# Cross-attention with layer norm on one core: one score visit for two row tiles, a cast moved to GpSimd, and a new order of the steady pairs

## The chip, the cores and the metric

The kernel runs on one core of a Trainium2 chip. Its engines work side by side, each through its own list of instructions in order: TensorE (PE in the profile) multiplies matrices and writes into the accumulation memory PSUM, of which a core has 8 banks; VectorE (DVE), ScalarE (ACT) and GpSimd (POOL) do elementwise work; SyncE (SP) issues most of the DMA transfers. Engines wait for each other through semaphores. The metric is the device time of one execution in microseconds.

## The reference

`x` holds 4 batches of 2048 rows of 512 numbers, `ctx_1024` 4 batches of 77 keys of 512 numbers. There are 16 heads of 32 columns.

```
q = x @ wq;  k = ctx @ wk;  v = ctx @ wv                  # split into 16 heads of 32
scores = q k^T / sqrt(32);  scores = where(mask, -inf, scores)
out = softmax(scores) v @ wo + x
result = (out - mean) / sqrt(var + 1e-5) * gamma + beta
```

Everything is float32. Products with the weight matrices are made from three products of split operands (a rounded high part and the rest, the low part): high by high, high by low, low by high.

## The kernel before

**Tiling.** The 8192 rows are 64 tiles `t` of 128 rows. Two tiles form a pair `n` (tiles 2n and 2n+1), four tiles form a group `g` of 512 rows, for which the transposed input is loaded (`load_xT`), cast to its high part (`cast_xT`, L166, on ScalarE, two casts of 128x1024 a group), and split into its low part (`split_xT`, L170, on GpSimd). `q_visit` (L180) makes a quarter of a group's queries: 12 matmuls of 512 columns into one PSUM bank, which `q_evac` (L194, VectorE) copies out.

**One tile's way.** `scores(t)` (L299) takes four banks and forms 16 heads x 128 rows x 77 keys by 32 small float32 matmuls (32 query columns deep, 64 rows wide; each shows as two instructions). `maxima` (L317) takes, on VectorE, one instruction per head that adds the mask, negates, takes the minimum and copies the scores from PSUM to `pbuf`. `exps` (L335, ScalarE) follows with one exponential per head, which also sums it. `recip` (L345, VectorE) and `normalise` (L350, GpSimd) divide. `transp` (L365, VectorE) turns 32x32 blocks into the buffer `B`, `regroup` (L387, SyncE) moves them by 12 transfers a pair into `PT`, `av` (L412, TensorE) multiplies by the values for a whole pair into two banks, `av_hi` (ScalarE) and `av_lo` (VectorE) split that product, `o_proj` (L502, TensorE, 12 matmuls of 512 columns) applies `wo` into one bank, `residual` (L520) and `moments` (L522, VectorE, then four small GpSimd operations L534 to L537) follow, then `scale` (L543, ScalarE), `affine` (L545, two GpSimd operations) and `store`.

**Order.** The order of all instructions on every engine is the order in which the program text issues them. Tiles 0 to 53 come from a loop (L714) whose turn makes one pair, `u` being its even tile. On TensorE a steady turn is: scores of tile u, `o_proj(u-6)`, a query visit, `av(n-2)`, scores of tile u+1, `o_proj(u-5)`, a query visit. Tiles 54 to 63 and everything left over come from the string `ORDER` (L46), a list of words that `do` (L844) executes one by one: a letter for the operation, a tile number, a part.

**PSUM.** `bank` (L98) hands out the 8 banks in a ring. A pair takes 14: four for each tile's scores, two for query visits, two for `av`, two for `o_proj`.

**The mask.** For each batch (8 pairs) `load_mask` and `mask_bias` make an additive mask in 96 columns from 77 by two VectorE operations, and `mask_min` and `mask_nan` (L289, L293) make a per-row epsilon `nz`, which is 1e-5 or, for a row whose keys are all masked, NaN. `moments` adds `nz` to the variance on GpSimd.

Of the kernel before, what the change touches and what calls it, by code (L numbers as in the profile page):

```python
# [31 lines left out]
GRP = 2 * BLK  # L32
MASKED = -3.0e38
EPS = 1.0e-5
WARM = 8
NPB = 3
KSCALE = 1.0 / HD**0.5
LATE = 48
CUT = 27
HALVES = [slice(0, D // 2), slice(D // 2, D)]  # L40

ORDER = """  # L46
# [22 lines left out]
def xattn_layernorm(  # L69
# [25 lines left out]

    ring, kept, rows, summed = [], set(), {}, set()

    def bank(name):  # L98
# [25 lines left out]
    unit = ident.bitcast(F32R)  # L124
    mhalf, mneg, gates = small[:, 0:2], small[:, 2:4], small[:, 4:5]
    last_st = small[:, 8:20].rearrange("p (n s) -> p n s", n=2)
# [24 lines left out]
    def keys_of(h):  # L151
        return slice(TAIL_K, NK2) if h % 2 == 0 else slice(0, NK)
# [10 lines left out]
    def cast_xT(g, c):  # L163
        if g not in gx:
            gx[g] = [sb.tile([P, NC_D, GRP], F32R, tag=t, name=f"{t}_{g}") for t in ("xth", "xtl")]
        nc.scalar.copy(gx[g][0][:, c : c + 2], fx[g, c])  # L166

# [109 lines left out]
    def load_mask(b):  # L277
        m8 = sb.tile([P, TPB, NK], U8, tag="m8", bufs=1, name=f"m8_{b}")
        nc.sync.dma_start(m8, mask[b])
        mb = sb.tile([P, TPB, NK2], BF16, tag="mb", name=f"mb_{b}")  # L280
        nz = sb.tile([P, TPB], F32, tag="nz", name=f"nz_{b}")
        bat[b] = (mb, nz, m8)

    def mask_bias(b, ts=slice(0, TPB)):
        mb, nz, m8 = bat[b]
        nc.vector.tensor_scalar(mb[:, ts, TAIL_K:], m8[:, ts], MASKED, None, ALU.mult)
        nc.vector.tensor_scalar(mb[:, ts, :TAIL_K], m8[:, ts, NK - TAIL_K :], MASKED, None, ALU.mult)

    def mask_min(b):  # L289
        mb, nz, m8 = bat[b]  # L290
        nc.vector.tensor_reduce(nz, m8, AX.X, ALU.min)

    def mask_nan(b):  # L293
        nz = bat[b][1]
        nc.vector.tensor_scalar(nz, nz, 3.0e38, 10.0, ALU.mult, ALU.mult)
        nc.vector.tensor_scalar(nz, nz, 0.0, EPS, ALU.mult, ALU.add)


    def scores(t):  # L299
        qs = qd[t // 4]  # L300
        nmax[t] = sb.tile([P, H], F32, tag="nm", bufs=3, name=f"nm_{t}")
        sums[t] = sb.tile([P, H], F32, tag="sum", bufs=3, name=f"sum_{t}")
        sc = scs[t] = [bank(f"sc_{t}_{j}") for j in range(GH)]
        for g in range(NG):
            for half in range(0, P, P // 2):
                for j in range(GH):
                    q = slice(HD * j, HD * (j + 1))
                    r0 = (t % 4) * P + half
                    nc.tensor.matmul(  # L309
                        sc[j][half : half + P // 2, g * NK : (g + 1) * NK],  # L310
                        qs[q, g, r0 : r0 + P // 2],
                        kct[q, g, t // TPB, keys_of(j)],
                        start=True,
                        stop=True,
                    )

    def maxima(t, lo, hi):  # L317
        pb = pbuf[t % NPB]
        mb = bat[t // TPB][0]
        nm = nmax[t]  # L320
        for h in HEADS[lo:hi]:
            g, j = divmod(h, GH)
            i = slot(h)
            nc.vector.tensor_tensor_reduce(  # L324
                pb[:, i // 2, (i % 2) * NK : (i % 2 + 1) * NK],
                scs[t][j][:, g * NK : (g + 1) * NK],
                mb[:, t % TPB, keys_of(h)],
                -1.0,
                3.0e38,
                ALU.add,  # L330
                ALU.min,
                accum_out=nm[:, i : i + 1],
            )
# [53 lines left out]
    def regroup(b):  # L387
        for n in range(12):
            regroup_part(b, n, nc.sync)
# [132 lines left out]
    def moments(t):  # L522
        b, tt = divmod(t, 2)
        st = sb.tile([P, 6], F32, tag="st", bufs=3, name=f"st_{t}")
        nc.vector.bn_stats(st, od[t])
# [4 lines left out]
        nc.vector.bn_aggr(mv[:, tt, :], st)  # L530
        nz = bat[t // TPB][1]
        if tt == 1:
            k = (t - 1) % TPB
            nc.gpsimd.tensor_tensor(rn[:, 0, :], mv[:, :, 1], nz[:, k : k + 2], ALU.add)  # L534
            nc.gpsimd.tensor_tensor(rn[:, 0, :], rn[:, 0, :], mhalf, ALU.pow)
            nc.gpsimd.tensor_tensor(rn[:, 1, :], mv[:, :, 0], rn[:, 0, :], ALU.mult)
            nc.gpsimd.tensor_tensor(rn[:, 1, :], rn[:, 1, :], mneg, ALU.mult)  # L537
# [50 lines left out]
    def rsqrt_one(t):  # L588
        mv = mvs[t, 1]
        k = t % TPB  # L590
        eps = bat[t // TPB][1][:, k : k + 1]
        if t in summed:
            nc.gpsimd.tensor_scalar(mv[:, 2:3], mv[:, 1:2], 1.0 / D, eps, ALU.mult, ALU.add)
        else:
            nc.gpsimd.tensor_tensor(mv[:, 2:3], mv[:, 1:2], eps, ALU.add)
        nc.gpsimd.tensor_tensor(mv[:, 2:3], mv[:, 2:3], mhalf[:, :1], ALU.pow)
# [35 lines left out]
    nc.gpsimd.memset(mhalf, -0.5)  # L632
    nc.gpsimd.memset(mneg, -1.0)
    for pb in pbuf:
        nc.gpsimd.memset(pb[:, :, 2 * NK :], 0.0)
# [57 lines left out]
    for m in range(0, NG, 2):  # L693
        keys_evac(pks, m)
    mask_min(0)
    for c in range(0, NC_D, 2):
# [16 lines left out]
    evac = [(0, 0)]  # L713
    for u in range(0, 2 * CUT, 2):  # L714
        n = u // 2
# [59 lines left out]
        if k == TPB - 4 and m + 1 < NB:  # L775
            mask_bias(m + 1)
        if k == TPB - 2 and m + 1 < NB:
            mask_min(m + 1)
            mask_nan(m + 1)

# [14 lines left out]
        if u == 0:  # L795
            mask_nan(0)
            split_wv()
            recip(0)
# [37 lines left out]
        "+": residual, "u": rsqrt_one, "y": centre, "z": finish, "k": scale, "f": affine, "w": store,  # L836
        "v": bias_one, "K": stretch, "G": shift, "p": pool_scale, "I": act_mean, "J": act_squares, "M": keep,
    }
# [5 lines left out]
    def do(op, k, part=0, queue="s"):  # L844
# [34 lines left out]

    for word in ORDER.split():  # L880
        op, (k, part) = word[0], (word[1:] + ".").split(".")[:2]
        queue = part[-1:] if part[-1:].isalpha() else ""
        do(op, int(k), int(part[: len(part) - len(queue)] or 0), queue or "s")

# [47 lines left out]
```

## Time and profile before

| | |
|---|---|
| Time, median of 3 runs (lowest, highest) | 514.41 us (514.13, 518.13) |
| Span of the profiled execution, first to last instruction | 510.7 us, 3.7 us less than the median of the runs |
| TensorE matmuls busy | 502.1 us |
| VectorE busy | 472.1 us |
| ScalarE busy | 471.2 us |
| GpSimd busy | 424.3 us |
| Mean granted TensorE clock | 0.996 |

The runs include what lies before the first and after the last instruction, the span does not; the 3.7 us are taken as fixed. Busy shares are means over the whole span; the stage that matters here is the loop over pairs.

### The profile page before, as it was taken

Reading aid. Unit: us, or ns where it says so; the run is one execution under the profiler, and the core shown is the slowest. Engines: PE = TensorE matmul, PEld = TensorE weight load, DVE = VectorE, ACT = ScalarE, POOL = GpSimd, SP = SyncE. Lnnn points to the kernel's source line nnn. Section 1 sums busy time; section 2 is a strip of 40 time slices with the busy share of each in tenths; the row PEclk is TensorE's granted clock in tenths of the full one; section 3 lists DMA queues with packets and bytes.
Section 4 is the critical chain, followed back from the end, with each engine's and each line's share of the span. In section 5 each row is a group of like instructions: output and inputs, shape, how many; then the busy total and the mean of one; then the engine's idle time right before and its main releaser. Section 6 shows DMA issues by size and latency. Waiting matters only on the chain.

```text
span 510.7 us, 20467 instructions
## 1 busy us (share of the span) xinstructions
PE 502.1 (98%) x6864; PEld 387.3 (76%) x6864; DVE 472.1 (92%) x2574; ACT 471.2 (92%) x2239; POOL 424.3 (83%) x382
## 2 busy tenths in 40 slices
PE   8999999999999999999999999999999999999994
PEld 6987777777777777777777777777777777777784
DVE  6798999899999888989999898889999989999997
ACT  6798999999899999999899999999899999999861
POOL 0659359988799988888989998898889989999894
PEclk9999999999999999999999999999999999999998
DMA  8946867888777888789777897788887778767665
GB/s 304 400 155 150 224 177 197 217 237 221 189 207 201 233 215 224 193 222 246 185 202 218 228 230 192 181 235 230 223 217 192 211 198 234 192 185 216 166 207 207
DMA packets 58280, 109.34 MB, mean 214 GB/s; under 512 B 9203, under 2 KB 10739, under 8 KB 58176
## 3 DMA queue, kind: packets, MB, share of 16 engines
q1 hardware_dynamic: 55776, 103.19, 73.1%
q0 software_dynamic: 1872, 4.20, 2.9%
q8 instruction: 55, 0.90, 0.8%
q10 hardware_dynamic: 528, 0.66, 0.4%
q14 instruction: 49, 0.40, 0.3%
HBM read 41.53 MB, written 16.78 MB: 114 GB/s over the span
## 4 chain that ended last, share of the span: by engine, by line
PE 87%; DVE 5%; DMA 4%; SPq 2%; POOL 1%; issue 1%; ACT 1%; DVEq 0%; POOLq 0%
PE pq L177 30%; PE po L517 29%; PE pa L419 10%; PE sc L309 10%; PE sc L517 3%; DMA PT<-B 2%; DVE B L373 2%; PE pv L243 2%; PE pk L203 1%; SPq L385 1%; DVE pbuf L324 1%; DMA stage_a<-wq 1%; PE pq L669 1%; POOL pbuf L350 0%; DVE q L194 0%
## 5 line engine op out<-in xcount | busy, mean ns | idle before, releaser
L339 ACT ACTIVATE pbuf<-pbuf,nm 128x77 f32<-128x77 f32 x1024 | 352.5, 350 | 15.0 <-DVE nm L324 13.6
L339 ACT ACTIVATION_READ_ACCUMULATOR pbuf<-pbuf,nm 128x1 f32 x1024 | 195.3, 191 | 0.0
L324 DVE CUSTOM_DVE_ANT_0 pbuf<-sc,mb 128x77 f32<-128x77 f32 x1020 | 169.9, 230 | 21.8 <-PE sc L309 21.5
L350 POOL TENSOR_TENSOR pbuf<-pbuf,ri 128x1232 f32<-128x1232 f32 x63 | 142.2, 2258 | 17.8 <-DVE ri L345 11.0
L177 PE MATMUL pq<-xth,wqh 128*128 128x512 f32 (+1 forms) x256 | 98.8, 386 | 0.0
L177 PE MATMUL pq<-xtl,wqh 128*128 128x512 f32 (+1 forms) x256 | 98.0, 383 | 0.0
L177 PE MATMUL pq<-xth,wql 128*128 128x512 f32 (+1 forms) x256 | 97.9, 383 | 0.0
L373 DVE STREAM_TRANSPOSE B<-pbuf 128x1280 f32<-128x1280 f32 x63 | 93.9, 1491 | 0.3
L517 PE MATMUL po<-woh,AH 128*128 128x512 f32 x224 | 93.3, 416 | 0.0
L517 PE MATMUL po<-wol,AH 128*128 128x512 f32 x224 | 87.7, 391 | 0.0
L517 PE MATMUL po<-woh,AL 128*128 128x512 f32 x224 | 86.7, 391 | 0.0
L324 DVE DVE_READ_ACCUMULATOR2_ANT nm<- 128x1 f32 x1024 | 83.2, 81 | 0.0
L547 POOL TENSOR_TENSOR o<-o,gam 128x512 f32<-128x512 f32 x53 | 69.9, 1319 | 14.4 <-ACT o L543 14.4
L548 POOL TENSOR_TENSOR o<-o,bet 128x512 f32<-128x512 f32 x53 | 68.4, 1290 | 4.2
L309 PEld LDWEIGHTS sc<-kct,q 32*64 32x64 f32 x4080 | 51.2, 130 | 23.7 <-issue 21.3
L170 POOL TENSOR_TENSOR xtl<-xtf,xth 128x1024 fp32r<-128x1024 f32 x28 | 67.1, 2398 | 0.0
L309 PE MATMUL sc<-kct,q 32*64 32x77 f32 x4080 | 61.2, 238 | 0.0
L419 PE MATMUL pa<-PT,vsb 96*32 96x256 f32 x960 | 58.2, 382 | 0.7 <-DMA PT<-B 0.3
L177 PEld LDWEIGHTS pq<-xth,wqh 128*128 128x128 f32 x256 | 48.1, 188 | 9.8
L177 PEld LDWEIGHTS pq<-xth,wql 128*128 128x128 f32 x256 | 48.1, 188 | 9.4
L177 PEld LDWEIGHTS pq<-xtl,wqh 128*128 128x128 f32 x256 | 48.1, 188 | 9.1
L517 PEld LDWEIGHTS po<-woh,AH 128*128 128x128 f32 x224 | 42.0, 188 | 12.0 <-DVE nm L324 0.4
(167 smaller groups left out, 707.5 us busy)
## 6 DMA issues: line engine op xcount, KB each, us to landing
PT<-B SPq DMA_DIRECT2D x355, 128.0 KB
xtf<-xT SPq DMA_DIRECT2D x28, 512.0 KB
o<-x SPq DMA_DIRECT2D x56, 256.0 KB
out<-o SPq DMA_DIRECT2D x56, 256.0 KB
PT<-B POOLq DMA_DIRECT2D x16, 128.0 KB, 5.2
o_end<-x SPq DMA_DIRECT2D x7, 256.0 KB
out<-o_end SPq DMA_DIRECT2D x7, 256.0 KB
xtf<-xT SPq DMA_DIRECT2D x4, 256.0 KB
```

The lines of the kernel that those rows point to most:

```text
L170: nc.gpsimd.tensor_tensor(l, fx.pop((g, c)), h.bitcast(F32), ALU.subtract)
L177: nc.tensor.matmul(pq, w[:, c, m * P : (m + 1) * P], r[:, c, rs], start=(n == 0), stop=(n == 11))
L243: nc.tensor.matmul(pv, ctx_s[c][i][:, r, :], v[c], start=(n == 0), stop=(n == 11))
L309: nc.tensor.matmul(sc[j][half : half + P // 2, g * NK : (g + 1) * NK], qs[q, g, r0 : r0 + P // 2], kct[q, g, t // TPB, keys_of(j)], start= ...
L324: nc.vector.tensor_tensor_reduce(pb[:, i // 2, (i % 2) * NK : (i % 2 + 1) * NK], scs[t][j][:, g * NK : (g + 1) * NK], mb[:, t % TPB, keys_ ...
L339: nc.scalar.activation(p, p, AF.Exp, bias=nmax[t][:, i : i + 1], scale=-1.0, accum_out=sums[t][:, i : i + 1])
L350: nc.gpsimd.tensor_tensor(pv, pv, rv.to_broadcast((P, NP, 2, NK)), ALU.mult)
L373: nc.vector.transpose(bt.rearrange("p c q r -> p q c r"), pbuf[t % NPB].rearrange("p q (c r) -> p q c r", c=5),)
L419: nc.tensor.matmul(pas[b, g // 2][HD * j : HD * (j + 1), (g % 2) * BLK : (g % 2 + 1) * BLK], vsb[:, 2 * b // TPB, HD * h : HD * (h + 1)], ...
L517: nc.tensor.matmul(pos[t][:, cols], a[:, c, rs], w[:, c, cols], start=go, stop=done)
L547: nc.gpsimd.tensor_tensor(o, o, gam, ALU.mult)
L548: nc.gpsimd.tensor_tensor(o, o, bet, ALU.add)
```

## The change

1. From pair 3 on (`JOIN` = 6 tiles, `CUT` = 27 pairs), 24 pairs no longer come from the loop but from a second string, `PAIR`, executed once a pair with tile and pair numbers relative to the pair. Pairs 0 to 2 keep the loop, tiles 54 to 63 keep `ORDER`, ahead of which stand three words, `JOINT`.
2. In these pairs the scores of both tiles are formed by `scores_pair` (word `S`) and `scores_rest` (word `D`), which follow one another on TensorE. They take six banks instead of eight: four banks `own` hold six 77-column blocks each, two banks `both` hold four each. `S` issues 48 of the 64 small matmuls, `D` the last 16. A pair takes 12 banks instead of 14.
3. On TensorE a pair is: S, D, `o_proj(2n-6)`, `o_proj(2n-5)`, two query visits, `av(n-2)`. The `av` product's second half and both low parts are taken at the start of the next pair.
4. For groups 4 and up the cast to the high part runs on GpSimd (`tensor_copy`), not on ScalarE.
5. The mask is brought to 96 columns on the host, `mask_bias` is one operation, `mask_min` and `mask_nan` are gone, and epsilon is a constant: `moments` adds it on VectorE with a `tensor_scalar` on 128x2 numbers instead of on GpSimd. A row whose keys are all masked now becomes NaN in another way: the cap on the minimum is 2.9e38 (`CEIL`) instead of 3.0e38, so that all its exponentials are zero and it is divided by a zero sum.

```diff
+PAIR = """
+q4 S L b-3.0 i4 a-3.1 T1.30 b-3.1 T0.1 D k-8 T0.2 T0.0 e0.1 e0.0 T1.31 f-8 O-6 x-3 w-8 T0.3 e0.3 B T1.10 e0.2 j4 O-5
++-6 T1.11 s-6 x-4 Q5 T1.1 r0 +-5 k-7 n0 T1.14 e1.11 s-5 e1.14 T1.3 Q6 f-7 q5 e1.1 g5 V-2 e1.15 t-1 t0 e1.10 e1.3 r1
+a-2.0 P-1 n1 w-7
+"""
+JOINT = """ a24.1 b24.0 b24.1 """
...
-        nc.scalar.copy(gx[g][0][:, c : c + 2], fx[g, c])
+        eng = nc.scalar.copy if g < 4 else nc.gpsimd.tensor_copy
+        eng(gx[g][0][:, c : c + 2], fx[g, c])
...
+    def score(t, g, j, half):
+        q = slice(HD * j, HD * (j + 1))
+        r0 = (t % 4) * P + half
+        return nc.tensor.matmul(
+            scs[t][g, j][half : half + P // 2],
+            qd[t // 4][q, g, r0 : r0 + P // 2],
+            kct[q, g, t // TPB, keys_of(j)],
+            start=True,
+            stop=True,
+        )
+
+    def scores_pair(b):
...
+        own = [bank(f"sc_{b}_{j}") for j in range(GH)]
+        both = [bank(f"sc_{b}_{j}") for j in ("e", "f")]
+        units = []
+        for j in range(GH):
+            mine = [(2 * b, g) for g in range(NG)] + [(2 * b + 1, g) for g in range(NG)]
+            for i, (t, g) in enumerate(mine):
+                bk, at = (own[j], i) if i < 6 else (both[j // 2], 2 * (j % 2) + i - 6)
+                scs[t][g, j] = bk[:, at * NK : (at + 1) * NK]
+            units.append(mine[6:] + mine[:6] if j % 2 == 0 else mine)
+        for i in range(6):
+            for half in range(0, P, P // 2):
+                for j in range(GH):
+                    score(*units[j][i], j, half)
+        held[b] = units
+
+    def scores_rest(b):
+        units = held.pop(b)
+        for i in (6, 7):
+            for js in ((0, 2), (3, 1)):
+                for half in range(0, P, P // 2):
+                    for j in js:
+                        score(*units[j][i], j, half)
...
-            nc.gpsimd.tensor_tensor(rn[:, 0, :], mv[:, :, 1], nz[:, k : k + 2], ALU.add)
+            nc.vector.tensor_scalar(rn[:, 0, :], mv[:, :, 1], EPS, None, ALU.add)
...
-    for u in range(0, 2 * CUT, 2):
+    for u in range(0, JOIN, 2):
...
-            tile_parts[op](k, q4 * part, q4 * part + q4)
+            lo, size = (q4 * part, q4) if part < 10 else (2 * part - 20, 2) if part < 20 else (part - 20, 1)
+            tile_parts[op](k, lo, lo + size)
...
+    for n in range(JOIN // 2, CUT):
+        pair(n)
+    for word in (JOINT + ORDER).split():
+        do(*read(word))
```

The words that the prediction uses: `T` maxima, `e` exponentials, `a` and `b` high and low part of the `av` product, `i` cast, `j` split, `r` reciprocal, `n` normalise, `t` transpose, `+` residual, `s` moments, `k` scale, `f` affine, `Q` and `q` query visit and its copy out, `V` the `av` product, `P` regroup, `w` store. A number after the letter is the tile's or pair's distance from the current one; a part of 0 to 3 means four heads, 10 to 17 two heads, 30 and up one head. `S`, `D`, `O`, `Q` and `V` run on TensorE; `T`, `b`, `+`, `s`, `r`, `t`, `q` on VectorE; `e`, `a`, `k` on ScalarE; `i`, `j`, `f`, `n` on GpSimd; `P`, `w`, `x`, `g` and `L` on SyncE's queue.

More of the change, by code (lines that the diff above doesn't have):

```diff
@@ L96, in xattn_layernorm @@
     ring, kept, rows, summed = [], set(), {}, set()
+    held = {}
     def bank(name):
@@ L306, in scores @@
                 for j in range(GH):
[L307 to L315, printed above, removed]
+                    score(t, g, j, half)
+    def score(t, g, j, half):
[9 more added lines that the diff above has]
+    def scores_pair(b):
+        for t in (2 * b, 2 * b + 1):
+            nmax[t] = sb.tile([P, H], F32, tag="nm", bufs=3, name=f"nm_{t}")
+            sums[t] = sb.tile([P, H], F32, tag="sum", bufs=3, name=f"sum_{t}")
+            scs[t] = {}
+        own = [bank(f"sc_{b}_{j}") for j in range(GH)]
[19 more added lines that the diff above has]
+                        score(*units[j][i], j, half)
     def maxima(t, lo, hi):
@@ L633, in xattn_layernorm @@
     nc.gpsimd.memset(mneg, -1.0)
+    nc.gpsimd.memset(meps, EPS)
     for pb in pbuf:
```

77 lines of the change are left out of this document (43 added, 34 removed).

## The prediction

> **What bounds the kernel now.** I read the page first: the busy shares, then the chain that ended last.
>
> ```profile
> span 510.7 us, 20467 instructions
> PE 502.1 (98%) x6864; PEld 387.3 (76%) x6864; DVE 472.1 (92%) x2574; ACT 471.2 (92%) x2239; POOL 424.3 (83%) x382
> PE 87%; DVE 5%; DMA 4%; SPq 2%; POOL 1%; issue 1%; ACT 1%; DVEq 0%; POOLq 0%
> ```
>
> TensorE holds 87% of the chain. The three others are 83% to 92% busy, so whoever takes work from TensorE soon meets another. The chain in order of time shows the loop from its first to its last score visit, with one query visit between:
>
> ```profile
> 59.80 0.88 PE sc L309 x54
> ...
> 206.84 2.72 PE pq L177 x12
> ...
> 404.21 0.88 PE sc L309 x53
> ```
>
> The score visit at 59.80 is that of tile 6, the one at 404.21 of tile 52: 344.41 us for 23 pairs, **14.974 us a pair**. The 24 pairs that the change rewrites are these and one more. Busy times by stretch, for one such pair between the starts of two `av` products (us; PE, PEld, DVE, ACT, POOL):
>
> ```profile
> 201.16:216.09 14.93, 14.93 (x212) 11.38 (x216) 13.42 (x79) 14.51 (x71) 13.18 (x12) 1.00 0.75 199
> ```
>
> TensorE is busy all of the 14.93, at a granted clock of 1.00. VectorE has 1.5 us to spare a pair, ScalarE 0.4, GpSimd 1.75. A shorter TensorE pair shortens the kernel until one of these, or a loop of waits, is met.
>
> **The change part by part.** *The score visit.* TensorE in order of time, around one visit:
>
> ```profile
> 209.17 0.39 PE L177 MATMUL pq<-xth,wql 128*128 128x512 f32 x1
> 209.49 0.95 PE L309 MATMUL sc<-kct,q 32*64 32x77 f32 x64
> 210.37 0.50 PE L517 MATMUL po<-woh,AH 128*128 128x512 f32 x1
> 210.71 0.39 PE L517 MATMUL po<-wol,AH 128*128 128x512 f32 x1
> ```
>
> A stream of 512-column matmuls takes 2.72 / 12 = 0.227 each. Without the visit the next would have started at 209.17 + 0.227 = 209.40; the stream is back in step at 210.71 - 0.227 = 210.48. The visit costs 1.08 us. Its 64 instructions start within 0.95 - 0.23 = 0.72 (0.23 being one of them), 11.4 ns each; the other **0.36 us** is entry and exit. Two visits a pair pay it twice, S and D together once: 128 instructions are issued as before. So TensorE's pair falls from 14.974 to 14.61, if D follows S without a gap. Bounds of the saving: 0.36 with no gap; 0 if D's wait drains the array and the entry is paid again. D shares bank `f` with S and waits there for the one-head maximum T1.30; that bank's share of S is issued in S's first third, so the maximum runs beside the rest of S. I take 0.36.
>
> [...]
>
> *The cast on GpSimd.* ScalarE loses one cast a pair. GpSimd's rows of one pair, from split to split, and rows that bound the new price:
>
> ```profile
> 199.37 2.40 POOL L170 TENSOR_TENSOR xtl<-xtf,xth 128x1024 fp32r<-128x1024 f32 x1
> 202.31 1.27 POOL L547 TENSOR_TENSOR o<-o,gam 128x512 f32<-128x512 f32 x1 [0.55 <-ACT o L543]
> 210.60 0.20 POOL L534 TENSOR_TENSOR rn<-mv,nz 128x2 f32<-128x2 f32 x1 [0.81 <-DVE mv L530]
> 210.88 0.70 POOL L535 TENSOR_TENSOR rn<-rn,small 128x2 f32<-128x2 f32 x1
> 214.30 2.40 POOL L170 TENSOR_TENSOR xtl<-xtf,xth 128x1024 fp32r<-128x1024 f32 x1
> ```
>
> ```profile
> L631 POOL MEMSET ident<- x1: 152/152/152, 0.7 to 0.7; 128x64 f32 x1
> L771 POOL MEMSET ident<- x1: 213/213/213, 26.1 to 26.1; 128x128 f32 x1
> L772 POOL TENSOR_SCALAR_AFFINE_SELECT ident<-ident x1: 293/293/293, 26.4 to 26.4; 128x128 fp32r<-128x128 f32 x1
> ```
>
> Without its two waits GpSimd's pair is 14.93 - 0.55 - 0.81 = 13.57; the epsilon add (L534, 0.28 to the next start) goes: 13.29, plus the cast `c`. No GpSimd cast is in the trace. From below, writing alone costs (213 - 152) / 64 = 0.95 ns an element over a fixed 0.09: 1.07 us for 1024. From above, the split, which reads two streams: 2.40. Between them the select, one stream in and one out, 293 ns for 128 elements: (293 - 91) / 128 = 1.58 ns, 1.71 us, if its fixed part were the memset's, which a longer setup would lower. I take **1.1**, next to the memset, since its write and a single read can run side by side. GpSimd's pair is then 14.4, and with some 0.25 of waiting for the epsilon, which now comes from VectorE, 14.65. It meets the old 14.974 at c = 1.43.
>
> [...]
>
> *The new loop of waits.* Rows of the same pair on TensorE, VectorE and ScalarE (between 210.57 and 211.78 stand eight maxima, with the reads of their results):
>
> ```profile
> 202.95 0.95 PE L309 MATMUL sc<-kct,q 32*64 32x77 f32 x64
> ...
> 203.89 0.24 DVE L324 CUSTOM_DVE_ANT_0 pbuf<-sc,mb 128x77 f32<-128x77 f32 x1 [1.40 <-PE sc L309]
> 204.23 0.36 ACT L339 ACTIVATE pbuf<-pbuf,nm 128x77 f32<-128x77 f32 x1 [0.34 <-DVE nm L324]
> ...
> 209.74 1.03 ACT L166 CAST xth<-xtf 128x1024 fp32r<-128x1024 f32 x1
> ```
>
> ```profile
> 207.63 0.68 DVE L520 TENSOR_TENSOR o<-po,o 128x512 f32<-128x512 f32 x1
> 208.23 1.50 DVE L373 STREAM_TRANSPOSE B<-pbuf 128x1280 f32<-128x1280 f32 x1
> 209.66 0.65 DVE L525 BATCH_NORM_STATS2 st<-o 128x6 f32<-128x512 f32 x1
> ...
> 210.44 0.22 DVE L345 RECIPROCAL ri<-sum 128x16 f32<-128x16 f32 x1
> 210.57 0.18 DVE L324 CUSTOM_DVE_ANT_0 pbuf<-sc,mb 128x77 f32<-128x77 f32 x1
> ...
> 211.78 0.69 DVE L194 COPY q<-pq 128x512 f32<-128x512 f32 x1
> 212.39 0.23 DVE L324 CUSTOM_DVE_ANT_0 pbuf<-sc,mb 128x77 f32<-128x77 f32 x1
> ```
>
> In the new order `q4`, at a pair's head, frees the bank into which S writes third, and stands on VectorE behind `r1`, which ends the pair. I follow it round from S. The first maximum starts after S's 96 instructions, 1.09, and 0.22 of tail (203.89 - 202.95 - 0.72): 1.31. The first exponential 0.34 later, 1.65. Sixteen exponentials run from 204.23 to 209.74, 5.51: 7.16, and r0 at 7.25. On VectorE then r0 0.13, residual 0.60, two maxima 0.30, moments 0.78, epsilon 0.15, four maxima 0.61, the copy q5 0.61, two transposes 2.86, r1 0.13, q4 0.69 (start to start from the rows above; a maximum is (211.78 - 210.57) / 8 = 0.15), and 0.1 to TensorE: 6.96. **The loop takes 14.2 us**, under TensorE's 14.61 by 0.4. ScalarE, 14.51 less 1.1, is no bound.
>
> One new instruction can lengthen it: the epsilon add, a `tensor_scalar` on 128x2. The trace has the like:
>
> ```profile
> L295 DVE TENSOR_SCALAR nz<-nz x4: 162/1288/1294, 29.1 to 368.8; 128x16 f32<-128x16 f32 x4
> ```
>
> ```profile
> 248.91 1.29 POOL L548 TENSOR_TENSOR o<-o,bet 128x512 f32<-128x512 f32 x1
> 248.94 1.29 DVE L295 TENSOR_SCALAR nz<-nz 128x16 f32<-128x16 f32 x1
> ```
>
> Once 0.16, but 1.29 where it started just after a GpSimd operation, until that one ended: it was held. In a pair the add comes 1.8 us after r0, and r0 releases the normalise of 2.26 us; it is held for what is left, some 0.5. Bounds: 0 if two elements aren't held, 2.26 if the normalise has just begun. With 0.5 the loop is 14.7, just past TensorE's 14.61. [...]
>
> *The rest* I cost at nothing. The dropped mask operations (some 3 us of VectorE in one pair of eight) lie under VectorE's 1.5 us of slack a pair and the next pairs'. The regroup's 12 transfers are issued at a pair's end instead of its middle, ahead of `w-7` on SyncE; the `av` product that needs them comes a pair later. If that cover failed, TensorE would stand before V. `a-3.1`, `b-3.0` and `b-3.1` stand before the first four maxima, but S takes 1.31 before these can start. Behind D's wait stand `O-6` and all later matmuls. Ahead of the tail stand two low parts (0.6 each) and a high part; one cast there moves to GpSimd; against that tile 53's exponentials are done earlier. I take 0, bounds -2 and +3.
>
> **Sum.** TensorE 14.61, the loop 14.7, GpSimd 14.65: I take 14.70, so 24 x (14.974 - 14.70) = 6.6 us. The profiled span of 510.7 becomes 504.1; with the 3.7 between span and median, **507.8 us**.
>
> **The rivals.** *GpSimd becomes the bound (slower).* If the cast costs 1.71, its pair is 13.29 + 1.71 + 0.25 = 15.25: 23 casts in these pairs x 0.28 = +6.4, 521 us. At the split's 2.40 it is 15.94: +22, 537. It decides from c = 1.43. For it: the split's 2.40 for 1024 elements is 2.3 ns an element. Against: it reads two operands.
>
> *The held epsilon add eats the gain.* If GpSimd runs a little late, the normalise starts later and the add is held for 0.8 to 1.3: the loop is 15.0 to 15.5, 515 to 527 us. It decides from 0.77. For it: GpSimd would be 98% occupied. Against: r0 itself releases the normalise, so the two keep their distance while GpSimd is on time.
>
> *The visit does not shrink.* D's wait costs what the second entry did: 14.97, no change, 514 us.
>
> **How the numbers follow.** A change of 1% (5 us) is about what a measurement of this kernel can tell from none. Chances: the forecast 0.52 (505 to 509.3, and down to 504 with all of the 0.36 and the tail's -2); the held add 0.18, half of it within 1%, the rest slower; the visit unchanged 0.10; GpSimd's bound 0.20, slower. Faster 0.52, same 0.25 with some of the forecast's edge going each way, slower 0.23. The range leaves out the dear half of the GpSimd case and little below: 504 to 521.
>
> **What would show it.** Right: one group of 128 small matmuls a pair, pairs of 14.6 to 14.75, a GpSimd cast of about 1.1, epsilon adds of 0.5 or more, ScalarE below 14. Wrong: TensorE idle before S (released by the copy `q`) for over 0.3 a pair, TensorE idle before a query visit on the split (GpSimd late), or a gap between S and D on VectorE's maximum.

## The result, and the profile after

The changed kernel takes **519.7 us** (median of 19 runs) beside 514.1 us for the kernel before on the same chips: a ratio of 1.011, 95% interval 1.009 to 1.014. It is slower, where the prediction had 507.8 and faster. The page of its profiled execution (522.1 us, one of the longer of the 19; 1.8 of it lie outside the span):

```profile
span 520.3 us, 20305 instructions
...
PE 503.0 (97%) x6864; PEld 394.2 (76%) x6864; DVE 482.7 (93%) x2581; ACT 453.6 (87%) x2215; POOL 445.4 (86%) x383
...
PE 46%; DVE 25%; ACT 10%; DMA 7%; SPq 7%; issue 3%; POOL 1%; DVEq 0%; ACTq 0%; POOLq 0%
```

TensorE held 87% of the chain before and holds 46% now; VectorE went from 5% to 25%. To see where the time is, three stretches are cut at score visits that both kernels have: that of pair 4 (tile 8) and that of tile 54. TensorE in order of time, the kernel before and then the changed one:

```profile
74.72 0.95 PE L309 MATMUL sc<-kct,q 32*64 32x77 f32 x64
...
419.07 0.94 PE L309 MATMUL sc<-kct,q 32*64 32x77 f32 x63
```

```profile
79.59 0.28 PE L311 MATMUL sc_e<-kct,q 32*64 32x77 f32 x1
...
424.53 0.39 PE L311 MATMUL sc<-kct,q 32*64 32x77 f32 x16
```

| us | before | forecast | after | after less forecast |
|---|---|---|---|---|
| up to the scores of pair 4 (start, junction) | 74.72 | 74.45 | 79.59 | 5.1 |
| 23 steady pairs | 344.35 | 338.1 | 344.94 | 6.8 |
| tile 54 to the end | 91.63 | 91.63 | 95.77 | 4.1 |
| span | 510.7 | 504.1 | 520.3 | 16.2 |

All three lose. Two neighbouring pairs from `av` to `av`, two stretches behind the junction (the place where the loop's last pair meets the first of the new ones), and one in the tail (busy times by stretch; us, then PE, PEld, DVE, ACT, POOL, the granted clock, DMA):

```profile
182.71:198.73 16.02, 15.03 (x209) 11.64 (x209) 15.48 (x81) 13.50 (x68) 15.28 (x13) 1.00 0.74 198
198.73:213.40 14.67, 14.67 (x210) 11.48 (x209) 14.12 (x80) 13.64 (x69) 13.94 (x12) 1.00 0.77 207
...
64.00:66.00 2.00, 2.00 (x16) 1.50 (x7) 1.89 (x25) 2.00 (x13) 2.00 (x2) 0.50 0.77 261
66.00:68.00 2.00, 2.00 (x6) 1.56 (x5) 0.61 (x8) 2.00 (x13) 1.45 (x1) 0.50 0.64 235
...
466.00:468.00 2.00, 2.00 (x9) 1.62 (x6) 1.97 (x19) 2.00 (x14) 2.00 (x2) 0.50 0.69 163
```

The second pair, 14.67 with TensorE busy throughout, is the forecast; the first, 16.02, is not: TensorE stands idle for 1.0. Some fifteen of the 23 are like the second. What TensorE waited for (in total, times, longest):

```profile
PE sc L311 <- DVE q L204: 2.6, 6, 1.0
PE sc L311 <- issue: 2.4, 2, 1.8
PE sc_f L311 <- DVE nm L354: 1.8, 1, 1.8
PE po L547 <- issue: 1.4, 1, 1.4
```

Before, its waits in these stretches came to under 0.5. Three things are new: six waits for the copy q4, one wait at the junction (D for the maximum T1.30), and idle times with no releaser ("issue"): 0.6 in the first new pair, 1.4 in pair 8, 1.8 in the tail. The granted clock, 1.00 at both places before, was 0.50 from 62.6 to 69.4 at the junction, where D waits until 63.5, and from 465.3 to 468.7 in the tail, where the stall of 1.8 ends at 465.5. How the long pair came about, on GpSimd, VectorE and TensorE in order of time:

```profile
173.25 1.05 POOL L176 CAST xth<-xtf 128x1024 fp32r<-128x1024 f32 x1 [1.52 <-DMA xtf<-xT]
...
179.24 2.25 POOL L380 TENSOR_TENSOR pbuf<-pbuf,ri 128x1232 f32<-128x1232 f32 x1
...
179.24 2.28 DVE L562 TENSOR_SCALAR rn<-mv 128x2 f32<-128x2 f32 x1
...
186.29 0.33 PE L311 MATMUL sc<-kct,q 32*64 32x77 f32 x8 [0.99 <-DVE q L204]
```

The cast waited for its load, GpSimd's normalise started late, and the epsilon add on two numbers lasted as long as that normalise, 2.28. VectorE then made q4 late, and TensorE waited. In all 24 pairs the add ends within 0.03 us of the end of the normalise beside it: it is held until then. Over all pairs (ns: least, median, most):

```profile
L562 DVE TENSOR_SCALAR rn<-mv x24: 383/817/2278, 74.3 to 419.5; 128x2 f32<-128x2 f32 x24
```

The groups of instructions give the same 24 adds in sum and mean (us, ns | idle time before):

```profile
L562 DVE TENSOR_SCALAR rn<-mv 128x2 f32<-128x2 f32 x24 | 23.9, 994 | 0.8
```

### The profile page after: what moved, and what is told of

It reads as the page before. It is cut to its first block, busy times and chain, and to the rows that moved or that the text cites. A ratio compares the mean times of both kernels' runs of the same rounds, so it can differ in the third digit from the quotient of the medians.

```text
span 520.3 us, 20305 instructions
## 1 busy us (share of the span) xinstructions
PE 503.0 (97%) x6864; PEld 394.2 (76%) x6864; DVE 482.7 (93%) x2581; ACT 453.6 (87%) x2215; POOL 445.4 (86%) x383
## 4 chain that ended last, share of the span: by engine, by line
PE 46%; DVE 25%; ACT 10%; DMA 7%; SPq 7%; issue 3%; POOL 1%; DVEq 0%; ACTq 0%; POOLq 0%
PE pq L187 16%; PE po L547 13%; ACT pbuf L369 9%; DVE B L403 8%; SPq L415 6%; DVE pbuf L354 5%; PE pa L449 4%; DMA PT<-B 4%; PE sc L311 3%; PE sc L547 3%; DVE q L204 3%; DVE AL L502 3%; DMA out<-o 2%; PE pv L253 2%; PE pk L213 1%
## 5 line engine op out<-in xcount | busy, mean ns | idle before, releaser
L354 DVE CUSTOM_DVE_ANT_0 pbuf<-sc,mb 128x77 f32<-128x77 f32 x828 | 141.0, 229 | 6.0 <-PE sc L311 5.5
L547 PE MATMUL po<-woh,AH 128*128 128x512 f32 x224 | 92.0, 411 | 1.4 <-issue 1.4
L403 DVE STREAM_TRANSPOSE B<-pbuf 128x1280 f32<-128x1280 f32 x63 | 91.7, 1483 | 0.2
L547 PE MATMUL po<-wol,AH 128*128 128x512 f32 x224 | 88.8, 397 | 0.0
L547 PE MATMUL po<-woh,AL 128*128 128x512 f32 x224 | 87.9, 397 | 0.1
L354 DVE DVE_READ_ACCUMULATOR2_ANT nm<- 128x1 f32 x1024 | 81.6, 80 | 0.0
L576 POOL TENSOR_TENSOR o<-o,bet 128x512 f32<-128x512 f32 x53 | 70.5, 1330 | 4.2
L311 PE MATMUL sc<-kct,q 32*64 32x77 f32 x3312 | 59.2, 239 | 5.2 <-DVE q L204 2.6
L547 PEld LDWEIGHTS po<-woh,AH 128*128 128x128 f32 x224 | 43.1, 192 | 12.6 <-issue 1.7
```

Of the source, the lines that this page charges most:

```text
L311: return nc.tensor.matmul(scs[t][g, j][half : half + P // 2], qd[t // 4][q, g, r0 : r0 + P // 2], kct[q, g, t // TPB, keys_of(j)], start=True,
L354: nc.vector.tensor_tensor_reduce(pb[:, i // 2, (i % 2) * NK : (i % 2 + 1) * NK], scs[t][g, j], mb[:, t % TPB, keys_of(h)], -1.0, CEIL, ALU ...
L403: nc.vector.transpose(bt.rearrange("p c q r -> p q c r"), pbuf[t % NPB].rearrange("p q (c r) -> p q c r", c=5),)
L547: nc.tensor.matmul(pos[t][:, cols], a[:, c, rs], w[:, c, cols], start=go, stop=done)
L576: nc.gpsimd.tensor_tensor(o, o, bet, ALU.add)
```

## The experiments

Each is named with its ratio to the kernel before on the same chip. "e1" and so on stand for the labels below.

### e1: the epsilon add back on GpSimd

```diff
-            nc.vector.tensor_scalar(rn[:, 0, :], mv[:, :, 1], EPS, None, ALU.add)
+            nc.gpsimd.tensor_tensor(rn[:, 0, :], mv[:, :, 1], meps, ALU.add)
```

(and `meps`, which holds the constant, is two columns wide)

> The changed kernel with one edit: the epsilon add of the moments goes back from VectorE to GpSimd, as in the kernel before. Theory (the held add is what makes some eight of the 23 steady pairs 15.1 to 16.1 us long): no VectorE operation of two numbers is held any more, GpSimd's pair becomes 13.29 + 1.04 + 0.28 = 14.61, the copy q4 comes on time, pairs come to 14.7 on average, and the time falls by (14.997 - 14.7) x 23 = 6.8 us, to some 513. Rival (the late loads of the transposed input make these pairs long by themselves, since GpSimd's split then comes late for the query visit): the late pairs stay at 15.1 or more and the time within 2 us of the changed kernel's 519.7. Second rival (GpSimd, now with both the cast and the add, becomes the bound): TensorE waits for the split and the time rises.

Measured: 514.3 us, ratio 1.002 (0.999 to 1.005): 5.4 us less than the changed kernel by the medians (4.9 by the ratios), so the first theory holds and both rivals fall. The two intervals together leave 3 to 7 us for it. TensorE's waits, and a pair by stretch:

```profile
PE sc L311 <- issue: 2.5, 2, 1.6
PE sc_f L311 <- DVE nm L354: 2.5, 1, 2.5
PE sc_f L311 <- issue: 1.2, 1, 1.2
...
PE po L547 <- issue: 0.8, 1, 0.8
...
PE sc_e L311 <- issue: 0.4, 1, 0.4
```

```profile
194.30:208.90 14.60, 14.60 (x209) 11.46 (x208) 13.62 (x79) 13.69 (x71) 14.14 (x12) 1.00 0.83 230
```

Every wait for q4 is gone. What is left in the pairs has no releaser. In order of time on TensorE, with the two cuts:

```profile
77.25 0.28 PE L311 MATMUL sc_e<-kct,q 32*64 32x77 f32 x1
...
93.99 0.28 PE L311 MATMUL sc_e<-kct,q 32*64 32x77 f32 x1 [0.41 <-issue]
...
139.26 0.50 PE L547 MATMUL po<-woh,AH 128*128 128x512 f32 x1 [0.79 <-issue]
...
345.41 0.28 PE L311 MATMUL sc<-kct,q 32*64 32x77 f32 x2 [0.96 <-issue]
...
390.79 0.28 PE L311 MATMUL sc_f<-kct,q 32*64 32x77 f32 x1 [1.18 <-issue]
...
418.74 0.32 PE L311 MATMUL sc<-kct,q 32*64 32x77 f32 x8
```

The 23 pairs take 418.74 - 77.25 = 341.5. The four with a stall (pairs 5, 8, 22, 25) take 15.3, 15.5, 15.8 and 16.1; the others 14.59 to 14.88, mostly 14.66. The four lose 4.0 us together. The pairs give 3.5 us of the gain against the first profile of the changed kernel, and 2.0 against its second (e11, 343.5 us); the rest of the 5 us is not in the pairs. In the traces it stands ahead of pair 4 and in the tail, where both executions of the changed kernel have the clock at half speed for 3.4 us and e1 has not. The tail holds none of the moved adds, so whether that part is their doing stays open.

### e2: the load a pair earlier

```diff
-            elif op in "gij":
+            elif op == "g":
+                for at in ((n + k, n + k + 1) if n == JOIN // 2 else (n + k + 1,)):
+                    if at < 2 * NGRP:
+                        do(op, at)
+            elif op in "ij":
```

> The changed kernel with one edit: the load of a group half's transposed input is issued one pair (15 us) earlier, at the same place of the order. Theory (in the late pairs the GpSimd cast waits for that load, which stands on SyncE's queue behind the regroup's twelve transfers; the normalise then runs late and the epsilon add is held behind all of it): no cast waits for a DMA any more, the holds stay at 0.5 to 0.7 us, pairs come to 14.7, and the time falls by 5 to 7 us, to 513 to 515. Rival (GpSimd is late for another reason, such as its own 14.4 us a pair): the casts start on time but the long pairs stay, and the time stays within 2 us of 519.7.

Measured: 518.7 us, ratio 1.008 (1.005 to 1.012), not told apart from the changed kernel's 1.011. No cast waits for a DMA any more, and the longest add is shorter, though e11, which lacks this edit, has no longer one (1.24):

```profile
L562 DVE TENSOR_SCALAR rn<-mv x24: 381/776/1230, 73.7 to 418.3; 128x2 f32<-128x2 f32 x24
```

The median hardly moved (0.82 to 0.78), so the usual hold of 0.6 stays, and the time with it: my theory for e2 falls. The late load explains the worst pair of the first profile, not the cost.

### e3: the first pair's output projection between S and D

```diff
+        words = PAIR.split()
+        if n == JOIN // 2:
+            words.remove("O-6")
+            words.insert(words.index("D"), "O-6")
```

> The changed kernel with one edit: in the first steady pair alone (pair 3) the output projection of tile 0 stands between S and D on TensorE, not behind D. Theory (at the junction from the loop to the pairs TensorE stands 1.78 us before D for a maximum that VectorE makes late, since it is still busy with the loop's last tiles; the granted clock then halves for 4 us; together some 5 us): TensorE has 2.7 us of work while VectorE catches up, the wait before D is under 0.3, the clock stays at 0.9 or more, and the time falls by 3 to 5 us, to 515 to 517. Rival (the junction's loss is VectorE's arrears, which only move): TensorE then waits as long further on, at the query visit or at the next pair's S, and the time stays within 1.5 us.

Measured: 519.2 us, ratio 1.010 (1.007 to 1.014). The wait before D went and came back within the next pair's S, so the rival holds:

```profile
79.31 0.51 PE L311 MATMUL sc<-kct,q 32*64 32x77 f32 x30 [1.75 <-DVE q L204]
```

### e4: the casts on ScalarE

```diff
-        eng = nc.scalar.copy if g < 4 else nc.gpsimd.tensor_copy
-        eng(gx[g][0][:, c : c + 2], fx[g, c])
+        nc.scalar.copy(gx[g][0][:, c : c + 2], fx[g, c])
```

(and the word `i4` behind `k-8`)

> The changed kernel with one edit: all casts of the transposed input stay on ScalarE, behind the scale of the tile four pairs back. Theory (the cast on GpSimd matters only through the late load: with the cast away GpSimd has 1.04 us to spare a pair, catches up after a late load, and the epsilon add is held for 0.7 or less): the late pairs shrink to 14.9 or less and the time falls by 3 to 6 us. Rival (ScalarE, at 13.6 + 1.0 with sixteen exponentials in the loop of waits, now delays that loop: the cast stands among the exponentials): the pair becomes some 14.2 + 0.5 + 1.0 = 15.7, and the time rises by up to 20 us.

Measured: 527.9 us, ratio 1.028 (1.023 to 1.033). The direction is the rival's, at under half its price:

```profile
PE sc L310 <- DVE q L203: 8.1, 7, 2.5
```

The waits for q4 are three times those of the changed kernel: with a cast among the exponentials the loop of waits runs over. The GpSimd cast is a part of the change that pays, in this order of work.

### e5: two score visits a pair

```diff
-... T0.1 D k-8 T0.2 T0.0 e0.1 e0.0 T1.31 f-8 O-6 x-3 ...
+... T0.1 k-8 T0.2 O-6 D T0.0 e0.1 e0.0 T1.31 f-8 x-3 ...
```

> The changed kernel with one edit: on TensorE the output projection of tile 2n-6 stands between S and D in every pair, so that a pair again has two visits of small matmuls (96 and 32) instead of one of 128. If the one visit is worth what the prediction gave it (0.36 us of entry and exit a pair), and TensorE bounds the good pairs, they go from 14.70 to 15.0 and the time rises by up to 24 x 0.36 = 8.6 us. If the loop of waits bounds the good pairs (the copy q4, the maxima and exponentials, the two reciprocals), the visit is free and the time stays within 2 us. If TensorE's stalls without a releaser (0.5 to 1.8 us, seen next to the 256 records of the merged visit) come from its length, they go, which is worth some 4 us the other way.

Measured: 555.6 us, ratio 1.081 (1.077 to 1.085), far outside all three expectations. Most pairs take 16.3. On TensorE and on VectorE:

```profile
193.32 0.33 PE L311 MATMUL sc<-kct,q 32*64 32x77 f32 x8 [1.05 <-DVE q L204]
...
197.67 0.24 DVE L354 CUSTOM_DVE_ANT_0 pbuf<-sc,mb 128x77 f32<-128x77 f32 x1 [1.80 <-PE sc_e L311]
```

VectorE waits 1.80 for the scores of D behind the projection, the exponentials follow late, and q4 with them. I had counted the visit's entry only; D lies on the loop of waits, and its place matters more than the entry. No pair has a stall without a releaser here; the tail has one of 2.4.

### e6: e1, e2 and e3 together

```diff
+ the edits of e1, e2 and e3
```

> The changed kernel with three edits at once: epsilon add on GpSimd, the load of the transposed input one pair earlier, and the first steady pair's output projection between S and D. Theory (late pairs from load and held add, and the junction, are where the forecast's 6.6 us went, some 7 and 5 us): pairs of 14.7 throughout, no clock drop at the junction, and 519.7 - 10 to 12 = 508 to 510 us, which is the forecast's 507.8 within its error. Rival (TensorE's stalls without a releaser and the tail cost the rest, or the parts overlap): 512 to 515.

Measured: 515.6 us, ratio 1.003 (1.000 to 1.006): no better than e1 alone. That is the rival's side, just above its 512 to 515. The early load adds nothing once the add is off VectorE; at the junction 1.1 us of idle time within pair 4's S took the place of 2.5 before D.

### e7 and e8: parts of the change in the kernel before

```diff
-        nc.scalar.copy(gx[g][0][:, c : c + 2], fx[g, c])
+        eng = nc.scalar.copy if g < 4 else nc.gpsimd.tensor_copy
+        eng(gx[g][0][:, c : c + 2], fx[g, c])
```

> The kernel before with one part of the change: the casts of groups 4 and up on GpSimd. Theory (TensorE bounds the pair at 14.97; GpSimd has 1.75 us of slack and takes 1.04): no change, within 1 us of 514. Rival (GpSimd's 13.57 + 1.04 + the waits of 1.36 is over 14.97, so that waits no longer fit): slower by up to 24 x 0.3 = 7 us.

```diff
-            nc.gpsimd.tensor_tensor(rn[:, 0, :], mv[:, :, 1], nz[:, k : k + 2], ALU.add)
+            nc.vector.tensor_scalar(rn[:, 0, :], mv[:, :, 1], EPS, None, ALU.add)
```

> The kernel before with one part of the change: the epsilon add on VectorE as a tensor_scalar (the masked rows' NaN is left out, so a row whose keys are all masked is computed otherwise). Theory (the add is held behind a GpSimd operation for up to its length, but VectorE has 1.5 us to spare a pair): holds of 0.2 to 2.3 us show, and the time stays within 2 us of 514. Rival (VectorE's maxima behind the held add come late and TensorE's next scores wait): slower by 5 us or more.

Measured: 1.001 (0.998 to 1.005) for the cast, 1.002 (0.999 to 1.006) for the add; neither is told from no change. The add of e8 shows next to no hold (ns):

```profile
L534 DVE TENSOR_SCALAR rn<-mv x24: 168/170/281, 76.2 to 419.9; 128x2 f32<-128x2 f32 x24
```

0.17 us in the old order, 0.82 in the new one. In e8's trace fifteen of the 24 adds have no GpSimd operation beside them; the others start in the last 0.3 us of one and end with it. The new order puts every add beside GpSimd's normalise. The expected holds did not show here, the expected time did.

### e9 and e10: the same kernel with its instructions shifted

The stalls of e1 come again in e2, e3 and e6 in the same pairs 5, 8, 22 and 25, each with nearly the same number of matmul records (instructions as the profile shows them, two to a small matmul) left in the visit (6 or 7, 0 or 1, 14, 7 or 8); e4 has three of the four. A place that is fixed in the list of instructions made me suspect their supply. The page of the changed kernel has two queues of the kind "instruction"; the larger (packets, MB, share):

```profile
q8 instruction: 54, 0.88, 0.8%
```

That is 16 KB a packet. The page does not say whose instructions it brings. If they are TensorE's, the 6864 matmuls and 6864 weight loads over 54 packets are 254 a packet; my estimate is 256, with a few that the profile does not count. So many the merged visit's 128 matmul records and their loads use up in 1.5 us (first record at 169.93, last at 171.45 in the first profile). Both kernels have the edit of e1, and form a few score matmuls twice, which only moves what follows: the first line, in `scores_pair`, stands in both, the other two, in `scores`, in e9 alone.

```diff
+        score(*units[1][0], 1, 0)
...
+        for j in range(2 if t < 5 else 0):
+            score(t, 0, j, 0)
```

> The kernel of e1 (epsilon add on GpSimd) with small score matmuls formed twice, which changes nothing but the place of all that follows in TensorE's list of instructions: one a pair in the steady pairs and ten in tiles 0 to 4 (11 ns each, some 0.4 us in all). Theory (TensorE's stalls without a releaser come from the supply of its instructions, which arrive in blocks of 16 KB, 256 instructions, 128 matmul records with their weight loads: a stall comes where a block ends 0 to 14 records before the end of the dense visit of 128 records; in e1 the stalled pairs 5, 8, 22, 25 have 6, 0, 14 and 7 records left, so a pair is some 422 instructions): a pair is now some 426.5 instructions, five thirds of a block, so only three places occur, 32, 75 and 117 records before the visit's end. No stall without a releaser in any of the 24 pairs, all of them at 14.6 to 14.8, and about 3.5 us less than e1 in the pairs; in the tail the stall of 1.6 us moves too, to an unknown place. Rival (the stalls hang on something else in pairs 5, 8, 22 and 25, such as other engines' transfers): they stay where they are and the time is e1's, 514.

> The same as e9 without the ten in tiles 0 to 4: one small score matmul formed twice in each steady pair, 4 instructions more a pair. Theory of the 16 KB blocks: the three places are now 10 to 12, 55 and 97 records before the visit's end, so every third pair stalls, at pairs 5, 8, 11, 14, 17, 20, 23 and 26, for 0.3 to 1.3 us each: eight stalls where e1 has four, and some 3 to 5 us more than e1 (517 to 519), though only 24 small matmuls of 11 ns were added. Rival: stalls at 5, 8, 22 and 25 as in e1, and 514 to 515.

Measured: e9 513.8 us, ratio 1.001 (0.999 to 1.003); e10 519.7 us, ratio 1.012 (1.009 to 1.015). TensorE's waits in e9:

```profile
PE sc_f L313 <- DVE nm L357: 2.5, 1, 2.5
...
PE pa L452 <- issue: 0.2, 1, 0.2
```

and the first two and the last of the stalls in e10:

```profile
97.02 0.28 PE L311 MATMUL sc<-kct,q 32*64 32x77 f32 x2 [0.76 <-issue]
...
142.41 0.28 PE L311 MATMUL sc<-kct,q 32*64 32x77 f32 x2 [0.85 <-issue]
...
412.96 0.28 PE L311 MATMUL sc<-kct,q 32*64 32x77 f32 x2 [0.59 <-issue]
```

In e10 the pairs 5, 8, 11, 14, 17, 20, 23 and 26 stall, as foretold, with 11 or 12 records left, for 0.34 to 0.85; in e9 no pair does. e10 has less added work than e9 and is 5.8 us slower. The rival falls. One stall is not of this kind: in pair 3, where by the same count a block ends 97 records before the visit's end, TensorE stalls for 0.53 in e10, as for 0.60 with 95 left in the first profile; e1, e2 and e11 have no stall there. The period agrees with the estimate: three pairs of some 426.5 instructions are 1280, five blocks of 256, and the stall comes in every third pair. Not as expected: e9 gained 0.5 us on e1, not 3.5. Its pairs take 14.75 instead of 14.66, for the matmul formed twice costs 0.09, not 0.01, and its junction had the clock drop.

### e11: the changed kernel once more

> The changed kernel itself once more, for what its first profile shows only once. If the halved clock at the junction (0.50 for 6 us there) and the single long stall of 1.43 us belong to the program, they come again at the same places. If they belong to that execution, the junction costs the 1.8 to 2.5 us of idle time before D alone, and the stalls sit at pairs 5, 8, 22 and 25 as in e1 to e3; the held epsilon adds and the waits for the copy q4 come again in either case.

Measured once: 520.2 us, with 79.01 up to pair 4, 343.51 in the pairs and 95.89 in the tail. The stalls stand at pairs 5, 8, 22 and 25 (0.66, 0.72, 0.79, 0.39) and in the tail (1.87), there again with the clock at 0.50 behind it; the clock at the junction stays at 1.00; the 16 us pair is not there, the longest being 15.7. So neither the halved clock at the junction nor that one pair comes in every execution. The adds are held again: median 0.81, mean 0.77, at most 1.24.

The waits for q4 are three here, 1.2 us in all, in pairs 7, 15 and 23. Each is the pair behind one in which VectorE has the operation on the mask (pairs 6, 14 and 22; 0.95 to 1.53 us). The first profile waits in pairs 7 and 15 too, and e2 there alone; e1, with the same mask operation, waits in none. So with the add held the loop of waits passes this operation on in seven of the nine cases of these three runs.

### e12: the shift with weight loads alone

The first two lines stand behind the program's first matmuls, the others behind D.

```diff
+    for i in range(32):
+        nc.tensor.ldweights(warm[:, :32])
...
+                for i in range(4):
+                    nc.tensor.ldweights(warm[:, :32])
```

> The kernel of e1 with weight loads that no matmul uses: 32 after the first matmuls of the program and 4 a steady pair, behind D. [...] Theory of the 16 KB blocks: weight loads shift the blocks just as matmuls do, the three places are 26, 69 and 111 records before the visit's end, no pair stalls, and if the loads run beside the matmuls the pairs stay at 14.70: 23 x 14.70 = 338 us instead of e1's 341.5, so some 3 us less than e1, about 511, which beats the kernel before (513) by 0.4 to 0.6%. Rival (the loads cost more, each draining the array): pairs of 14.8 or more and 514 or more. In both cases the junction keeps its 2.5 us of idle time, with or without the clock drop behind it (some 2 us).

Measured: 512.6 us, ratio 0.9985 (0.9963 to 1.0006). In order of time, and behind the junction by stretch:

```profile
79.30 0.28 PE L311 MATMUL sc_e<-kct,q 32*64 32x77 f32 x1
...
418.75 0.32 PE L311 MATMUL sc<-kct,q 32*64 32x77 f32 x8
```

```profile
66.00:68.00 2.00, 2.00 (x6) 1.51 (x6) 1.22 (x16) 2.00 (x13) 2.00 (x1) 0.50 0.92 339
```

The time lies between the theory's 511 and the rival's 514. No pair stalls; the 23 take 339.45, 2.0 less than in e1 (3.5 were expected; a load costs some 0.02 by estimate, 339.45 less e1's 341.5 - 4.0 without its stalls, over 92 loads). The tail is 510.3 - 418.75 = 91.55, that of the kernel before. From pair 3's S to pair 4's it takes 19.15 us, 1.7 more than in e1, with the clock at 0.50.

### e13 and e14: the junction

Both add to e12. The first edit stands in both, the second in e14 alone.

```diff
-        eng = nc.scalar.copy if g < 4 else nc.gpsimd.tensor_copy
+        eng = nc.scalar.copy if g < 3 else nc.gpsimd.tensor_copy
```

```diff
-        if u:
+        if u and u + 2 < JOIN:
             recip(u + 1)
             normalise(u + 1)
...
+            if word == "T0.1" and n == JOIN // 2:
+                recip(u - 1)
+                normalise(u - 1)
```

> The kernel of e12 with the GpSimd cast from group 3 on instead of 4: two more casts (1.03 us each, one ahead of the exponentials of tile 4, one behind those of tile 5) leave ScalarE for GpSimd, which stands idle for 3.6 and 4.4 us there. If ScalarE's arrears set the junction (in e1 and e12 the exponentials of tile 5 end at 62.7, and the reciprocal, the copy q4, the first maximum and D follow them), these exponentials end near 61.7, D starts 1 us earlier, the next exponentials 1.0 to 1.3 us earlier, and S of pair 4 comes 1.0 to 1.3 us earlier than e12's 79.3, or some 3 us earlier if the clock drop behind the shorter idle time stays away: 1 to 3 us less than e12. If the scores and maxima of tile 5 set the end of its exponentials (ScalarE waits for VectorE there), nothing changes: within 1 us of e12's 512.6.

> The kernel of e13 with one more edit: on VectorE the reciprocal of tile 5 (and with it its normalise on GpSimd) stands behind the copy q4 and the first five maxima of pair 3, not ahead of them. If VectorE's order sets the junction, D no longer waits for more than 0.7 us (VectorE has a transpose until 62.1 before), the clock stays at 1.00, S of pair 4 comes at 75 to 76.5 instead of 79.3 and the time falls by 3 to 4 us against e12, to 508.5 to 509.5. If ScalarE's arrears set it, D's wait goes but TensorE stands idle before S of pair 4 for the copy q4 by some 1 to 2 us, as in e3, and the time is e13's within 1 us.

Measured: e13 512.9 us, ratio 0.999 (0.997 to 1.001), e12's. Its exponentials of tile 5 end 0.7 us earlier than in e12 (62.5 instead of 63.2), but so does all before them in this execution (pair 3's S starts at 59.44 instead of 60.15): the moved casts did not bring them forward. ScalarE then waits 1.23 for VectorE, and D still waits 2.5. So the second expectation holds, and the casts on ScalarE are not what sets the junction. e14: 511.1 us, ratio **0.9963 (0.9941 to 0.9985)**, faster than both kernels.

```profile
62.60 0.33 PE L311 MATMUL sc_f<-kct,q 32*64 32x77 f32 x1 [1.60 <-DVE nm L354]
...
77.64 0.28 PE L311 MATMUL sc_e<-kct,q 32*64 32x77 f32 x1
...
416.69 0.32 PE L311 MATMUL sc<-kct,q 32*64 32x77 f32 x8
```

D waits 1.60 instead of 2.55, not the 0.7 expected; the idle time before pair 4's S that ScalarE's arrears would have brought is not there; the clock dropped here too (0.50 from 62.7 to 66.1). The time lies between the two expectations. VectorE's order is one part of the junction's price: the 0.7 us for which the reciprocal waited for the exponentials, and the reciprocal itself, no longer stand ahead of q4. What is left of D's wait is VectorE's own work: in e14's trace it goes from one operation to the next (the maxima of tile 5, a low part, a transpose of 1.5, q4) until T1.30 at 62.3. That taking this work away would end the wait was not tried; e3, which gave TensorE other work in its place, met the wait one pair on.

## Why the prediction was wrong, point by point

**The visit, the cast and GpSimd: right.** Pairs without a disturbance take 14.66 in e1 with TensorE busy throughout, so one visit instead of two saves 14.97 - 14.66 = 0.31, against 0.36 forecast. The cast takes 1.04, against 1.1: no more than the 1.07 worked out from the memsets for writing alone, so its single read adds nothing that shows. GpSimd is busy for 14.1 of 14.6 in e1, and TensorE never waits for a split in the pairs. The rival in which GpSimd becomes the bound did not come, nor the visit that does not shrink.

**The step that failed first: a loop of waits without slack was priced as if nothing disturbed it.** The mechanism was right, and so was the usual pair: I had the loop at 14.7 with a hold of "some 0.5", and fifteen of the 23 pairs take 14.64 to 14.83. With 0.17 of its own, the add's median of 0.82 is a hold of 0.65, so the loop stands at TensorE's time and has no room left. I took 14.70 for every pair; the eight others take 15.07 to 16.13. One of them (pair 8) is a stall of supply; the others show disturbances that such a loop passes on: the mask operation of every eighth pair, the late load, adds held for 1.1 to 1.4. "The rest I cost at nothing" counted the mask operations that go, and not the one that stays in the loop. The hold costs some 5 us (e1; 3 to 7 by its interval), of which the traces show 2.0 to 3.5 in the pairs. Why GpSimd runs late was also guessed wrongly at first: the loads explain the worst pair, not the cost (e2).

The rival "the held epsilon add eats the gain", given 0.18, names this cause, and its time (515 to 527) holds the result. That it does is in part luck. Its condition, a hold over 0.77, is met by the mean of the first profile (0.99 less 0.17, 0.8) and not by that of e11 (0.6); and some 5 us on the forecast's 507.8 make 513, below its range. The other 7 us came from terms that neither it nor the forecast had.

**"The rest I cost at nothing": three terms were missing.** *The supply of instructions* costs 4.0 us in e1's pairs and, with a stall of 1.6, 1.8 in its tail (e1, e9, e10, e12). I wrote that "128 instructions are issued as before" and did not ask how fast they must arrive. *The junction* costs 2.5 to 4.9 us (pair 4's scores at 77.25 to 79.59 instead of 74.72), the dearer where the clock falls. D's wait behind T1.30 was named, but looked at only in the steady pair, where S hides it; in the first one VectorE still finishes tile 5. *The tail* was given -2 to +3 and came to +4.1. It holds a stall of 1.79 and 3.4 us at half clock, some 1.7 us of TensorE's time by estimate (half of 3.4); with the stall and without the clock drop it is +1.8 (e1), with neither it is +0 (e12).

**The 3.7 us between span and median** were 1.8 around the span, as the changed kernel's execution shows (522.1 and 520.3); the rest was the spread of the runs. With 1.8 the forecast would have been 505.9, further off.

**The sum.** The time is 11.9 us over the forecast. By the medians e1 takes away 5.4, e12 another 1.8, e14 another 1.4; the last two steps are each within the intervals of the ratios, and rest on the traces. e14's span, 508.3, stands 4.2 over the forecast's 504.1: 3.2 up to pair 4 (77.64 less 74.45; some 1.7 of it the clock), 1.0 in the pairs (339.05 less 338.1), nothing in the tail.

## What to carry to other kernels

When a loop of waits and an engine come out within 0.1 us of each other, forecast the sum of their disturbances, not the time of the usual turn: follow the operations that come only in some turns round the loop too. A two-number operation counts by what may hold it: the add here took 0.82 at the median, 0.17 of it its own. Where a change packs many small instructions together, compare the instructions needed in a stretch (here 256 in 1.5 us) with the size of a block of their supply (here 256 by estimate), and look for idle time without a releaser that recurs at a fixed place in the list. A change of order has a price at the seam with the old one (here 2.5 to 4.9 us), which has to be followed there and not in the steady state.

## What the runs showed that I had not expected

**TensorE can stall near the end of a block of instructions.** In the pairs TensorE stalls for 0.3 to 1.4 us where, by the count of e9 and e10 and the estimate of 256 instructions, a 16 KB block ends 0 to 14 records before the end of a dense visit; the tail's stalls are 0.7 to 2.4, with 9 or 10 records left. Four unused weight loads a pair, which cost some 0.02 each, move the pairs out of that window (e12, e14). That the next block comes late is inferred from these places; no view shows it. It is not the whole of it: e13, with the same loads, has one stall of 0.31 with 25 records left, and pair 3 stalled in two executions with 95 and 97 left.

**The clock falls after short idle times, sometimes.** Around 1.6 to 2.6 us without a matmul at the junction the granted clock was 0.50 in the first profile and e10 (for 6.8 us) and in e9, e12 and e14 (for 3.4), and it stayed at 1.00 there in e1, e2, e4, e11 and e13; the length of the idle time does not separate them. Where it falls for 3.4 us, pair 4 comes some 1.7 us later (19.1 us from pair 3's S instead of 17.5), for 6.8 some 2.7 to 3.0.

What separates them is where the idle time lies. Within one execution the drops start at multiples of 3.41 us from each other (62.55 and 465.33 in the first profile are 118 such steps apart) and last one or two steps. At the junction, the step ahead of a drop holds 1.5 to 2.6 us in which TensorE is idle. In e1, e2, e11 and e13 the wait of 2.5 is split between two steps, at most 1.3 in either (there the place of the steps is read from the drop at the end of the execution). Over the traces of all runs, behind the first 25 us, each step at full clock with 1.69 us or more idle was followed by a drop and none with less than 1.48 (in the first profile 1.48 ahead of 62.55 and 1.63 ahead of 465.33, each with a drop, and 1.22 from 141.05 without); between them both occur, and e4's 1.61 at the junction is such a case without a drop.

**One matmul more costs four times its share of the visit.** A small score matmul formed twice lengthens the pair by 0.09 us (14.75 in e9, 14.66 in e1), though the visit issues one every 23 ns (two records of 11.4). The runs show the price and not its reason.
